# A wait on every indirect DMA of a slot of node rows, instead of on the first of the slot alone

## The chip, the cores and the metric

One core of one Trainium2 chip. The time is the device time of one execution in microseconds (us); less is better. The engines are named as in the profile: PE (TensorE), DVE (VectorE), ACT (ScalarE), POOL (GpSimd) and SP (SyncE).

## What is computed

Sixteen graphs of 1,024 nodes with 64 channels each pass two graph layers. In the first, some edges of a node of high degree are left out, every node sorts, channel by channel, the features of its remaining neighbours and of itself, and a weighted sum of three quantiles of the sorted list (at 0.25, 0.5 and 0.75) is its aggregate. The second is three dense graph convolutions. Both are added to their input after a layernorm. Cut to the core (`neigh` is `adj > 0` without the diagonal):

```python
h = relu(layernorm(x))
# layer 0
rem = neigh & (skip > 1) & (rank % skip == skip - 1) & mask    # then made symmetric
nd = where(rem, 0, adj_with_diagonal) > 0
s = sort(where(nd[..., None], h[:, None], inf), axis=2)
nv = nd.sum(2)
for tau, w in ((.25, .25), (.5, .5), (.75, .25)):
    agg += w * (s interpolated at position tau * (nv - 1))
x = x + (relu((h + agg) @ W1 + b1) @ W2 + b2) * mask
# layer 1
h = relu(layernorm(x))
x1, x2, x3 = bn(relu(adj @ (h @ Wi) + bi)), one after the other
x = x + relu(concat(x1, x2, x3) @ Wl + bl)
```

## The kernel before

The graphs are worked in eight pairs. Within a graph the nodes are put in order of their number of neighbours ("place"), so that nodes of like degree stand together and share one sorting network. Places 0 to 640 and 960 to 1,024 are worked with the channels of two graphs on the partitions (blocks, `BLOCKS` and `TAIL`); PE picks the neighbours' rows by products with selection matrices (L1176, L1247). Places 640 to 960, the **node sets** (`NODES`), are worked with the nodes on the partitions, and their neighbours' rows are fetched from DRAM by indirect DMAs. This is where the change lies.

**A node set.** `fetch_nodes` (its indirect DMA is L1361) makes one tile `g_nodes` of 128 partitions by `slots` x G x 64 values, with G = 2 in every set. There are 17, 19 or 21 slots, a slot being one neighbour of each of 128 nodes, and a slot is filled by two indirect DMAs of 128 rows of 64 values (a = 0 and a = 1). In sets of kinds 0 and 1 the two are the two graphs of a pair; in kind 2 (21 slots) they belong to two different pairs. There are 20 sets and 744 such gathers in all, all issued on POOL's queue. `sort_nodes` then sorts the set on DVE (`quantiles`, L1092 for the min and max steps, L1104 for the products with the coefficients) and the aggregates are stored to DRAM (`agg_d`).

**The condition.** `quantiles` writes the sort operation that it has just put into the program to `sorted_by[0]` (at L1092). `ask()` in `fetch_nodes` adds, to the gather with a = 0 of each slot, a dependency on that operation: the gather may start only when that sort step is done. The gather with a = 1 has no such dependency. The first set's 34 gathers are asked for before there is any sort, and have none.

**What sets the order.** The program is written as generators. `weave` runs one sort and steps other generators beside it, each in a given stretch of the sort (`asking(nodes, 0.0, 0.9)`: its slots are asked for, evenly, over the first 90% of the sort's work). So the source places a gather between certain sort operations. A scheduler then sets the order on each engine: an instruction that waits for nothing may be placed ahead of those in front of it in the source. Sections under `tc.high_priority()` go ahead of others once what they need is there: the sends of image rows (L895, 8 for each graph), the loads of those rows (L910) and the aggregate loads (L1554). On a queue the instructions are issued in the order so set, one after the other.

**The loop over pairs** (about 250 to 2,000 us). For each pair: sort of block 0, a node sort, sort of block 1, sort of block 2, a node sort, at times tails, sort of the last block. Two node sets are fetched and sorted for each pair. Beside the sorts run the gathers of the next block on PE and the preparation of the next pair (`prepare`), in which ACT and PE compute the edges and the places, and POOL sends the image rows (L895) to their places and loads them back (L910).

**The late part** (about 2,000 us to the end). While the last pair's sorts are worked, `later` runs beside them. For each pair p, `load(p)` loads the input, h and the aggregates: the last by 16 indirect DMAs on POOL (L1554), from `agg_d` into the tile `agg`, of which there is one buffer. It is free for the next pair once the layernorm of the pair before (L608) has been transposed on PE (L1440). `first` adds h (L1451, on DVE) and works the dense part of layer 0; `second` the three convolutions (L1509). In this part four node sets are fetched ahead of their sorts (`then`), beside the sorts of blocks 1 and 2, the tails and a node sort.

Of the kernel before, what the change touches and what calls it, by code (L numbers as in the profile page):

```python
# [408 lines left out]
def graph_layers_kernel(ctx: ExitStack, tc: tile.TileContext, ins, out: bass.AP):  # L409
# [641 lines left out]
    sorted_by = [None]  # L1051
# [296 lines left out]
    def fetch_nodes(pairs, i, pools, tag):  # L1348

        work, ps, rows = pools  # L1350
        j0, j1, _, slots = NODES[i]
        G = len(pairs) if i == 2 else 2
        pool = work if tag == "s" else keep if tag == "r0" else rows
        g = pool.tile([P, slots, G * C], F32, tag=tag, bufs=2 if tag == "s" else 1, name="g_nodes")

        def ask():
            for k in range(slots):
                for a in range(G):
                    st = pairs[a if i == 2 else 0]
                    at = 4 if i == 2 else 2 * a + i  # L1360
                    asked = nc.gpsimd.indirect_dma_start(  # L1361
                        out=g[:, k, a * C : (a + 1) * C],
                        out_offset=None,
                        in_=rows_d[st.p][:, :],
                        in_offset=bass.IndirectOffsetOnAxis(ap=st.listed[:, at, k : k + 1], axis=0),
                    )
                    if a == 0 and sorted_by[0] is not None:
                        tc.add_manual_dep(
                            asked.ins, sorted_by[0].ins.name,
                            mybir.DependencyInfo(mybir.DependencyClass.Sync, mybir.DependencyReason.DATA),  # L1370
                            reason="rows are asked for one by one",
                        )
                yield

        z = work.tile([P, len(TAUS), G], F32, tag="z_nodes", bufs=2, name="z_nodes")
        for a in range(G):
            st = pairs[a if i == 2 else 0]
            at = 4 if i == 2 else 2 * a + i
            nc.scalar.copy(z[:, :, a : a + 1], st.nodes_z[:, :, at : at + 1])
        return pairs, i, g, z, Steps(ask())  # L1380

    def asking(fetched, first, end, share=1.0):
# [509 lines left out]
```

## Time and profile before

| | before |
|---|---|
| median of 3 runs | 2845.74 us (2841.83 to 2846.65) |
| the profiled execution's own time | 2855.05 us |
| its span | 2853.2 us |
| mean granted clock of PE | 0.869 |
| node gathers (L1361) on POOL | 744, busy 979.2 us, mean 1,316 ns |
| image rows sent (L895) on POOL | 128, busy 178.7 us, mean 1,396 ns |
| aggregate loads (L1554) on POOL | 128, busy 134.8 us, mean 1,053 ns |
| first addition of a late pair (L1451) on DVE | 8, busy 9.8 us, idle before them 184.1 us |

The profile is one execution. Times are in us from the start of its span. A line of a timeline gives the start, the duration, the engine, the source line, the operation, the tile written and the tiles read, and in square brackets the time that the engine was idle before it and what ended that idle time; "issue" means that nothing shown in the profile was waited for. A line of the waits gives engine, tile and line, what was waited for, the sum in us, how often, and the longest. In the slices, the span is cut into 40 equal parts, and each digit is the busy share in tenths. The span lies 1.9 us below the execution's own time.

### The profile page before, as it was taken

How to read it: one execution, taken by the hardware profiler on the slowest of the kernel's cores; microseconds unless marked ns; L12 is line 12 of the kernel's file. 1: busy time of each engine (PE TensorE's matmuls, PEld its weight loads, DVE VectorE, ACT ScalarE, POOL GpSimd, SP SyncE). 2: the span in 40 equal slices, each digit the busy share in tenths (PEclk: the TensorE clock that was granted, in tenths of full speed). 3: DMA queues.
4: the chain of work that ended last, by engine and by line, in shares of the span. 5: the costliest groups of instructions: out<-in, count | busy, mean ns of one | idle time of the engine just before them, and what ended most of it. 6: DMA issues, size and time to landing. Idle time of an engine off the chain costs nothing. (4 is left out here: it accounts for less than half of the span.)

```text
span 2853.2 us, 54558 instructions
## 1 busy us (share of the span) xinstructions
PE 2127.4 (75%) x21226; PEld 1374.2 (48%) x21226; DVE 2259.9 (79%) x5356; ACT 1657.8 (58%) x3324; POOL 1358.7 (48%) x1155
## 2 busy tenths in 40 slices
PE   1567986897798699779855986997588496448768
PEld 0344563564455365545523553665355363234445
DVE  3117999889899989989999999989688486647843
ACT  2686788678677858867773777687423141122222
POOL 5115363475526416443734274175646748862220
PEclk9788997998899799789878997998798798778989
DMA  3303222322422323142431222322310351221221
GB/s 96 109 30 98 80 88 65 104 80 58 107 72 86 81 91 91 46 110 68 98 65 45 82 86 73 112 75 61 80 21 19 74 82 51 42 56 39 48 61 46
DMA packets 261035, 205.27 MB, mean 72 GB/s; under 512 B 217120, under 2 KB 217248, under 8 KB 256672
## 3 DMA queue, kind: packets, MB, share of 16 engines
q1 hardware_dynamic: 165120, 131.39, 15.5%
q0 software_dynamic: 39680, 62.23, 9.1%
q10 hardware_dynamic: 55968, 8.09, 2.1%
q8 instruction: 168, 2.75, 0.4%
q14 instruction: 99, 0.81, 0.1%
HBM read 148.82 MB, written 52.75 MB: 71 GB/s over the span
## 5 line engine op out<-in xcount | busy, mean ns | idle before, releaser
L1361 POOL DMA_INDIRECT g_nodes<-rows_d,rows_listed x744 | 979.2, 1316 | 952.5 <-DVE prod L1104 276.2
L1176 PE MATMUL pg<-s,hp 128*64 128x496 fp8e4 (+5 forms) x8064 | 747.0, 337 | 134.9 <-ACT hp L697 56.1
L1176 PEld LDWEIGHTS <-hp 128*64 128x64 bf16 x8064 | 450.2, 113 | 376.9 <-ACT hp L697 67.2
L1509 PE MATMUL pg<-adjT,xw 128*64 128x512 fp8e4 x2304 | 282.5, 394 | 24.6 <-ACT xw L1498 11.4
L895 POOL DMA_INDIRECT live_d<-edge,place x128 | 178.7, 1396 | 191.1 <-DVE place L887 154.9
L1151 DVE TENSOR_SCALAR s<-r 128x3200 uint16<-128x3200 uint16 (+2 forms) x192 | 199.6, 1049 | 56.9 <-PE pg L1176 56.8
L1554 POOL DMA_INDIRECT agg<-agg_d,place x128 | 134.8, 1053 | 196.4 <-DMA agg_d<-agg_nodes 118.0
L1509 PEld LDWEIGHTS <-xw 128*64 128x64 bf16 x2304 | 135.4, 113 | 154.1 <-issue 22.8
L782 ACT ACTIVATE edge<-a 128x1024 fp8e4<-128x1024 uint32 x128 | 135.8, 1062 | 105.1 <-DMA a<-in_adj 87.2
L1180 ACT ACTIVATE g<-pg 128x400 f32<-128x400 f32 (+3 forms) x168 | 84.3, 502 | 191.1 <-PE pg L1176 161.3
L1092 DVE TENSOR_TENSOR t<-g 128x800 f32<-128x800 f32 (+9 forms) x184 | 168.0, 926 | 5.4 <-ACT g L1180 3.4
L884 ACT ACTIVATE stays<-keys,minus 128x1024 fp8e4<-128x1024 f32 x128 | 143.6, 1122 | 41.7 <-PE keys L876 40.5
L865 ACT ACTIVATE edge<-q,bias 128x1024 fp8e4<-128x1024 f32 x128 | 142.2, 1112 | 41.6 <-PE q L860 41.6
L838 ACT ACTIVATE stays<-cs,back 128x1024 f16<-128x1024 f32 x128 | 139.1, 1114 | 41.5 <-DVE look L819 19.8
L789 PE MATMUL ptE<-ident_h,one 128*128 128x128 bf16 x1024 | 83.4, 232 | 106.1 <-DVE one L786 58.0
L1092 DVE TENSOR_TENSOR g<-t 128x992 f32<-128x992 f32 (+7 forms) x176 | 160.0, 934 | 2.4
L1451 DVE TENSOR_TENSOR agg<-agg,h_late 128x1024 f32<-128x1024 f32 x8 | 9.8, 1224 | 184.1 <-DMA agg<-agg_d,place 184.1
L930 PE MATMUL pt<-ident_h,lp 128*128 128x128 bf16 x1024 | 107.7, 276 | 60.7 <-ACT liveT L933 33.2
L1247 PE MATMUL pg<-s,hp 128*64 128x384 bf16 (+14 forms) x1872 | 149.1, 301 | 2.8 <-DVE s L1216 2.7
L792 ACT ACTIVATE edgeT<-ptE 128x1024 fp8e4<-128x1024 f32 x128 | 130.8, 1033 | 19.9 <-PE ptE L789 19.6
L1513 ACT ACTIVATE xT<-pg,c_L_gnn_b 128x512 f32<-128x512 f32 x48 | 32.9, 686 | 183.9 <-PE pg L1509 175.3
L786 DVE TENSOR_SCALAR one<-a 128x1024 fp8e4<-128x1024 f32 x128 | 88.5, 696 | 55.6 <-DMA a<-in_adj 45.3
(253 smaller groups left out, 5043.3 us busy)
## 6 DMA issues: line engine op xcount, KB each, us to landing
a<-in_adj SPq DMA_DIRECT2D x128, 512.0 KB
adjT_d<-edgeT SPq DMA_DIRECT2D x16, 1024.0 KB
lp<-live_d POOLq DMA_DIRECT2D x32, 512.0 KB
adjT<-adjT_d SPq DMA_DIRECT2D x16, 1024.0 KB
g_nodes<-rows_d,rows_listed POOLq DMA_INDIRECT x744
room<-in_x SPq DMA_DIRECT2D x16, 256.0 KB
h_d<-room SPq DMA_DIRECT2D x16, 256.0 KB
rows_d<-room SPq DMA_DIRECT2D x64, 64.0 KB
```

What stands on the lines that cost most here:

```text
L782: nc.scalar.activation(edge[:, t, :], a[:, :].bitcast(U32), AF.Sign, accum_out=found[:, 0, b, t : t + 1], saturate=False)
L838: nc.scalar.activation(stays[:, t, :], cs, AF.Abs, bias=back[:, t : t + 1], scale=2.0)
L865: nc.scalar.activation(edge[:, t, :], q, AF.Relu, bias=bias(-2.0), accum_out=nv[:, t : t + 1], saturate=False)
L884: nc.scalar.activation(junk, keys, AF.Sign, bias=minus[:, t : t + 1], accum_out=above[:, t : t + 1], saturate=False)
L895: sent = nc.gpsimd.indirect_dma_start(out=live_d[b][:, :], out_offset=bass.IndirectOffsetOnAxis(ap=place[:, b, t : t + 1], axis=0), in_=ed ...
L1092: sorted_by[0] = nc.vector.tensor_tensor(view(bufs, o, n1, n2), view(bufs, a, n1, n2), view(bufs, b, n1, n2), ALU.max if op else ALU.min)
L1151: nc.vector.tensor_scalar(s[:, j, :, us, :], st.r[0][:, :, us, j0:j1], abs(k - 3), 0x0808, ALU.logical_shift_right if k > 3 else ALU.logic ...
L1176: summed = nc.tensor.matmul(out=pg[x * C : (x + 1) * C, those, :], lhsT=st.hp[:, part, x, u, :], rhs=picked, start=(i == 0 and part == 0), ...
L1247: summed = nc.tensor.matmul(out=pg[x * C : (x + 1) * C, ks, w0:], lhsT=st.hp[:, part, x, u, :], rhs=s[:, ks, x, u, w0:], start=(whole and ...
L1361: asked = nc.gpsimd.indirect_dma_start(out=g[:, k, a * C : (a + 1) * C], out_offset=None, in_=rows_d[st.p][:, :], in_offset=bass.IndirectO ...
L1509: nc.tensor.matmul(out=pg[cs, :], lhsT=part[:, u, cs], rhs=adjT[x][:, u, sl], start=(u == 0 and k == 0), stop=(u == NT - 1 and k == len(xw ...
L1554: nc.gpsimd.indirect_dma_start(out=agg[:, t, x, :], out_offset=None, in_=agg_d[b][:, :], in_offset=bass.IndirectOffsetOnAxis(ap=place[:, b ...
```

## The change

The condition `a == 0` is dropped. Both gathers of a slot, not only the first, get the dependency on the sort operation that stands ahead of them in the source.

```diff
--- before.py
+++ after.py
@@ -1364,7 +1364,7 @@
                         in_=rows_d[st.p][:, :],
                         in_offset=bass.IndirectOffsetOnAxis(ap=st.listed[:, at, k : k + 1], axis=0),
                     )
-                    if a == 0 and sorted_by[0] is not None:
+                    if sorted_by[0] is not None:
                         tc.add_manual_dep(
                             asked.ins, sorted_by[0].ins.name,
                             mybir.DependencyInfo(mybir.DependencyClass.Sync, mybir.DependencyReason.DATA),
```

The instructions themselves are the same in number and kind. Their order is the same on PE, DVE, ACT and SP, and differs on POOL, where the gathers with a = 1 no longer stand ahead of their partners. Between two groups of image rows (L895) there are, in turn, 62 and 10 gathers in the program before, and 52 and 20 in the changed one. Ahead of the eight groups of aggregate loads (L1554) stand, each counted from the group before it (the first from the last load of image rows, L910):

| group of 16 loads | 1 | 2 | 3 | 4 | 5 | 6 | 7 and 8 |
|---|---|---|---|---|---|---|---|
| gathers ahead, before | 28 | 14 | 62 | 27 | 82 | 15 | 0 |
| gathers ahead, changed | 14 | 28 | 51 | 21 | 83 | 31 | 0 |

## The prediction

> **What bounds the kernel now.** I read the page first (engine totals, slices), then VectorE's waits, then the timelines of POOL and VectorE (DVE) around each wait. Totals and slices:
>
> ```profile
> PE 2127.4 (75%) x21226; PEld 1374.2 (48%) x21226; DVE 2259.9 (79%) x5356; ACT 1657.8 (58%) x3324; POOL 1358.7 (48%) x1155
> ...
> DVE  3117999889899989989999999989688486647843
> ```
>
> A slice is 71.3 us. From the fourth to the twenty-sixth (about 210 to 1,850 us) DVE is 80 to 90% and more busy: the loop over pairs is bound by its sorts. From the twenty-eighth on it falls to 40 to 80%. Its waits say why:
>
> ```profile
> DVE agg L1451 <- DMA agg<-agg_d,place: 184.1, 8, 61.5
> DVE s L1151 <- PE pg L1176: 56.8, 27, 5.8
> ```
>
> Eight waits, 184.1 us, all after 2,030 us: VectorE stands before the first addition of each late pair (L1451) until that pair's 16 indirect loads (L1554) have landed. Those loads and the 744 node gathers share POOL's queue, in program order. So in the tail the question is how many gathers stand ahead of a pair's loads. The two views that price this are POOL's timeline around the fourth pair's loads, and DVE's at the waits:
>
> ```profile
> 2325.02 0.97 POOL L1361 DMA_INDIRECT g_nodes<-rows_d,rows_listed  x1 [31.65 <-PE pg L1247]
> ...
> 2352.41 1.09 POOL L1361 DMA_INDIRECT g_nodes<-rows_d,rows_listed  x1 [0.30 <-issue]
> 2353.80 0.94 POOL L1554 DMA_INDIRECT agg<-agg_d,place  x1 [0.30 <-issue]
> ```
>
> ```profile
> 2052.76 1.23 DVE L1451 TENSOR_TENSOR agg<-agg,h_late 128x1024 f32<-128x1024 f32 x1 [18.78 <-DMA agg<-agg_d,place]
> ...
> 2273.74 1.22 DVE L1451 TENSOR_TENSOR agg<-agg,h_late 128x1024 f32<-128x1024 f32 x1 [37.58 <-DMA agg<-agg_d,place]
> ...
> 2375.39 1.22 DVE L1451 TENSOR_TENSOR agg<-agg,h_late 128x1024 f32<-128x1024 f32 x1 [22.71 <-DMA agg<-agg_d,place]
> ...
> 2531.51 1.22 DVE L1451 TENSOR_TENSOR agg<-agg,h_late 128x1024 f32<-128x1024 f32 x1 [61.54 <-DMA agg<-agg_d,place]
> ```
>
> In the first, 17 gathers (2325.0 to 2353.5) run one behind the other, gap 0.30, and the load starts right behind them: the number in brackets is the idle time before an instruction. In the second, the brackets are the stalls. Sixteen loads take 19.7 us (2353.80 to 2373.47) and 22.9 to 25.5 where DVE works beside them.
>
> In the loop the place to read is the start of a node sort: DVE must find all slots there.
>
> ```profile
> 759.53 1.41 POOL L1361 DMA_INDIRECT g_nodes<-rows_d,rows_listed  x1 [16.68 <-DVE g L1092]
> ...
> 776.30 1.19 POOL L1361 DMA_INDIRECT g_nodes<-rows_d,rows_listed  x1 [0.30 <-issue]
> ```
>
> ```profile
> 786.38 1.48 DVE L1092 TENSOR_TENSOR t_nodes<-g_nodes 128x1280 f32<-128x1280 f32 x1
> ```
>
> Eleven gathers, released at 759.3 and done at 777.5; their sort begins at 786.38 without a wait. No wait of DVE on a node gather is in the trace.
>
> **What the skill says.** "Perfetto Trace Analysis", section on SWDGE DMA instructions: the recorded end is the last descriptor, not the data. The trace agrees: loads ended on POOL at 2050.94, DVE went on at 2052.76, 1.8 us later. "DMA: Bandwidth & Descriptors", Anatomy of one DMA: a wait is served by the issuing sequencer before dispatch, so what stands behind on that queue waits too; the 0.30 us gap above agrees. "GPSIMD Engine Reference", Key points: GpSimd shares its SBUF interface with VectorE. The trace agrees: gathers with their gap come at 1.25 us while DVE is idle (32 of them, 2470.3 to 2510.2), at 1.66 while it sorts (759.5 to 777.8), up to 1.93 (2373.8 to 2470.3). No page bears on the order that the scheduler makes.
>
> **The change part by part.** It adds a condition to 372 of the 744 gathers (the second of each slot), less 34 issued before any sort. No instruction is added or removed, and PE, DVE, ACT and SP keep their order. A second gather directly behind its first, on the same queue, waits for nothing new: price nothing by itself. What counts is that POOL's order changes. Before, the scheduler moved the free second gathers ahead in bursts (62 gathers between two sets of image rows, then 10; after, 52 and 20); now each slot's two stand together behind their sort operation.
>
> *(a) Image rows (L895) in the loop.* The even image's come behind 10 fewer gathers, some 11 to 16 us earlier; nobody was late for them. The odd image's wait for their places (L887) either way. Nothing.
>
> *(b) Node sorts in the loop.* The burst ahead is gone, so after the last conditions two gathers per slot are to come.
> - Fifth set (21 slots, sort at 786.4): 22 instead of 11 gathers from 759.5. In 26.9 us at 1.66, 16.2 are done; 5.8 are left while DVE stands, at 1.25: 7.2, and 1.8 to land: **+9.0**.
> - Tenth set (21 slots): POOL is the bound, 42 gathers back to back. The free ones began at 1324.3; the first condition ends at 1328.8. So 4.5 later: 1407.5 + 4.5 + 1.8 = 1413.8 against a sort at 1410.7: **+3.1**.
> - 17-slot sets at 1801.4 and 1555.8: 18 gathers instead of 9. For the first, 1801.4 + 18 x 1.7 + 1.8 = 1833.8 against its first reader of the last slot at 1832.65, and a little for its partner: **+2** for both.
> - The other sets have 1 to over 8 us left by the same sum: 0.
>
> Loop: +14 (from +4, if gathers keep 1.25 and only the fifth and tenth sets are late at half, to +22 at a pace of 1.93).
>
> *(c) The tail*, as shift D of DVE against before, without the loop's:
> 1. First loads: 14 instead of 28 gathers ahead; the last two slots' conditions end by 2018.6, the gathers by 2022.8. Sixteen loads beside a working DVE, 21.5, and 1.8 to land: 2046.1 against 2052.8: D = -6.7.
> 2. The 21-slot set sorted at 2086.65: 22 instead of 11 gathers, condition at 2064.9 - 6.7 = 2058.2, sort due at 2080.0. In 21.8 us at 1.685, 12.9 are done; 9.1 x 1.25 = 11.4, landing 1.8: 2093.2. D = +6.6; this step costs 13.3.
> 3. Second loads hang on the sort itself: D stays.
> 4. Third loads: 51 instead of 62 gathers ahead. The 52nd of before starts at 2238.56; there the loads now begin: 2238.6 + 6.6 + 19.7 + 1.8 = 2266.7 against 2273.74: D = -7.0. The stall of 37.6 becomes 24.
> 5. Fourth loads: the 17 hoisted gathers shown above are gone (counted from the start of the tail 131 gathers stood ahead, now 114). The one buffer agg is free once the layernorm's last step (L608, done at 2334.2) is transposed (L1440), 1.4 later; with D that is 2328.6. Loads 23.8 beside DVE, and 1.8: 2354.2 against 2375.39: D = -21.2. The stall of 22.7 becomes 9.
> 6. Fifth loads: 83 against 82 gathers, POOL back to back: D = -20. The stall stays at 61.
> 7. Sixth loads: 31 instead of 15 gathers ahead, from 2510.5 at 1.515 (2530 to 2553): 2557.5, where they would be ready at 2568.6 - 20 = 2548.6. D = -11.1.
> 8. Seventh and eighth hang on sorts and on their own stores: D stays -11.
>
> Where stalls go: DVE finds work earlier, but the pairs' matmuls (L1509) follow in a fixed row, so I carry D on unchanged.
>
> Sum: +14 - 11 = **+3 us**. The profiled run's own time is 2855.05 (span 2853.2); it becomes 2858. The median of the runs shown is 2845.74, 9.3 below the profiled one; I take the same 3 us from it: **2849**.
>
> **Unknowns, both ends.** The trace of before shows no two-gather burst with DVE reading behind it. Its price lies between nothing (all hidden by work that follows) and 9 + 3 + 2 + 13 = 27 us as worked, 33 at the slowest pace; a gain in the loop is excluded, since no DVE wait on a gather exists there. Landing: 1.8 taken; the larger burst might need 3.
>
> **Rivals.** A measurement of this kernel tells about 0.2% (5.7 us) from no change.
> - *A, the tail's gain stands alone.* The node sorts' lateness is swallowed: DVE has some 3 us of other idle time in every 50 of the loop, which a stall can displace. Then -11, and without step 2 as well -11 - 13 = -24: 2822 to 2835, say 2828. For it: 26% of L1361's idle time hangs on DVE (276.2 of 952.5 us at one line), POOL is 48% busy. Against it: 22 gathers cannot be done in 26.9 - 1.8 = 25.1 us unless each takes 1.14, and the fastest stretch shows 1.25. Chance 0.27.
> - *B, slower: gathers late at every sort behind the first block sort.* The point from which it decides is the pace: 18 gathers between 1801.4 and 1830.9 need 1.64 each. At 1.93, with the doubled burst against a sorting DVE, the fifth set is late by 12, the tenth by 5, and five of the 17- and 19-slot sets by 3 to 4 each: +34; the tail's step 2 costs 15: D = -9. Sum +25: 2871. For it: the paces of 1.92 and 1.75 at those two places (gathers of several us at 1519 to 1547). Against it: 1.58 to 1.66 at 324, 525 and 759. Chance 0.25.
> - *C, the order is not changed at all.* Excluded: POOL's instruction order differs (first burst 62 against 52). Chance 0.
>
> **Chances.** Forecast case 0.48, own range 2837 to 2863; within it about 0.08 faster, 0.20 same, 0.20 slower by that bound. With A and B: faster 0.35, same 0.20, slower 0.45. The range takes in A's middle and B's, and leaves out their ends: 2824 to 2869.
>
> **What would show it.** Right: POOL's timeline shows gathers in twos behind each condition; DVE waits on g_nodes appear (none before), about 9 us at the fifth set and 13 at the set of 2086; L1451's third wait is 24, the fourth 9, the fifth still 61, the sixth about 21. Wrong: no DVE wait on g_nodes (A), or such waits at eight sets or more (B); a fourth wait still near 23 would mean that the loads were not held by the hoisted gathers.

## The result and the profile after

The change makes the kernel slower: 2871.09 us (median of 4 runs, 2867.16 to 2889.58) against 2843.78 (4 runs, 2840.71 to 2846.65). The medians lie 27 us apart; the ratio is 1.0101, with an interval of 1.0067 to 1.0135, which is 19 to 38 us. The forecast was 2849, 3 us slower, with a range of 2824 to 2869. The measured time lies 2 us above that range and the loss is nine times the forecast; the time came out at that of rival B.

The two profiles stand closer than the medians. The changed kernel's profiled execution took 2867.16 (span 2865.3), 4 under its median; that of the kernel before took 2855.05, 11 over its own. Their difference is 12.1. Both numbers are needed below: stalls are read from the traces, the size of an effect from the runs.

The engine totals and DVE's waits of the changed kernel:

```profile
PE 2137.9 (75%) x21226; PEld 1380.6 (48%) x21226; DVE 2262.7 (79%) x5356; ACT 1657.4 (58%) x3324; POOL 1363.2 (48%) x1155
```

```profile
DVE agg L1451 <- DMA agg<-agg_d,place: 160.7, 8, 67.8
...
DVE t_nodes L1092 <- DMA g_nodes<-rows_d,rows_listed: 36.1, 5, 14.7
...
DVE g_nodes L1092 <- DMA g_nodes<-rows_d,rows_listed: 1.1, 1, 1.1
```

Every engine is as busy as before to within 0.5% (DVE 2262.7 against 2259.9); what has moved is idle time. The wait of the late pairs' additions fell from 184.1 to 160.7. In its place stands a wait that the profile before does not have at all: node sorts wait 37 us for their rows. The three longest of these, in DVE's timeline:

```profile
795.29 1.49 DVE L1092 TENSOR_TENSOR t_nodes<-g_nodes 128x1280 f32<-128x1280 f32 x1 [10.01 <-DMA g_nodes<-rows_d,rows_listed]
...
1613.34 1.23 DVE L1092 TENSOR_TENSOR t_nodes<-g_nodes 128x1024 f32<-128x1024 f32 x1 [8.24 <-DMA g_nodes<-rows_d,rows_listed]
...
2117.33 1.49 DVE L1092 TENSOR_TENSOR t_nodes<-g_nodes 128x1280 f32<-128x1280 f32 x1 [14.66 <-DMA g_nodes<-rows_d,rows_listed]
```

And what was won, at the third and fourth pair's additions, with the fifth that grew:

```profile
2289.58 1.25 DVE L1451 TENSOR_TENSOR agg<-agg,h_late 128x1024 f32<-128x1024 f32 x1 [23.62 <-DMA agg<-agg_d,place]
...
2380.87 1.23 DVE L1451 TENSOR_TENSOR agg<-agg,h_late 128x1024 f32<-128x1024 f32 x1 [10.27 <-DMA agg<-agg_d,place]
...
2542.98 1.29 DVE L1451 TENSOR_TENSOR agg<-agg,h_late 128x1024 f32<-128x1024 f32 x1 [67.84 <-DMA agg<-agg_d,place]
```

The brackets were 37.58, 22.71 and 61.54 before. Since DVE runs the same instructions in the same order in both kernels, the start of one and the same instruction can be subtracted between two traces; each jump of this difference is a place where time was lost or won. The shift is +22 when the first late addition is due, +30.7 after the sort at 2117, +15.8 after the third addition, +5.5 after the fourth, +11.5 and +16.2 after the fifth and sixth, and +12 to +13 at the end.

How the first long wait comes about is seen in POOL's timeline at the fifth set, where DVE stands from 785.3 to 795.3:

```profile
785.43 0.94 POOL L1361 DMA_INDIRECT g_nodes<-rows_d,rows_listed  x1 [0.30 <-DVE coef L1104]
...
791.67 0.94 POOL L1361 DMA_INDIRECT g_nodes<-rows_d,rows_listed  x1 [0.30 <-issue]
```

The gathers follow each other with the same gap of 0.30, and six of them were still to come when DVE had nothing left to do: the queue, not the last condition, is late (DVE had finished its last sort step, the last that a condition can name, at 778.9). From 785.4 on, with DVE idle, each takes 0.94; the last ends at 792.6, and 2.7 later the sort begins.

### The profile page after: what moved, and what is told of

It is laid out like the page before. It is cut to its first block, busy times and chain, and to the rows that moved or that the text cites. A ratio compares the mean times of both kernels' runs of the same rounds, so it can differ in the third digit from the quotient of the medians.

```text
span 2865.3 us, 54544 instructions
## 1 busy us (share of the span) xinstructions
PE 2137.9 (75%) x21226; PEld 1380.6 (48%) x21226; DVE 2262.7 (79%) x5356; ACT 1657.4 (58%) x3324; POOL 1363.2 (48%) x1155
## 3 DMA queue, kind: packets, MB, share of 16 engines
q1 hardware_dynamic: 165120, 131.39, 15.5%
## 5 line engine op out<-in xcount | busy, mean ns | idle before, releaser
L1361 POOL DMA_INDIRECT g_nodes<-rows_d,rows_listed x744 | 1005.9, 1352 | 979.8 <-DVE g L1092 298.7
L895 POOL DMA_INDIRECT live_d<-edge,place x128 | 157.5, 1231 | 168.7 <-DVE place L887 126.0
L1554 POOL DMA_INDIRECT agg<-agg_d,place x128 | 134.2, 1049 | 213.1 <-DMA agg_d<-agg_nodes 59.4
L1092 DVE TENSOR_TENSOR t_nodes<-g_nodes 128x256 f32<-128x256 f32 (+6 forms) x192 | 124.7, 659 | 39.8 <-DMA g_nodes<-rows_d,rows_listed 36.1
L1451 DVE TENSOR_TENSOR agg<-agg,h_late 128x1024 f32<-128x1024 f32 x8 | 9.9, 1242 | 160.7 <-DMA agg<-agg_d,place 160.7
```

Of the source, the lines that this page charges most:

```text
L895: sent = nc.gpsimd.indirect_dma_start(out=live_d[b][:, :], out_offset=bass.IndirectOffsetOnAxis(ap=place[:, b, t : t + 1], axis=0), in_=ed ...
L1092: sorted_by[0] = nc.vector.tensor_tensor(view(bufs, o, n1, n2), view(bufs, a, n1, n2), view(bufs, b, n1, n2), ALU.max if op else ALU.min)
L1361: asked = nc.gpsimd.indirect_dma_start(out=g[:, k, a * C : (a + 1) * C], out_offset=None, in_=rows_d[st.p][:, :], in_offset=bass.IndirectO ...
L1554: nc.gpsimd.indirect_dma_start(out=agg[:, t, x, :], out_offset=None, in_=agg_d[b][:, :], in_offset=bass.IndirectOffsetOnAxis(ap=place[:, b ...
```

## The experiments

Theory: the loss is node sorts that stand for their last rows (first fifteen sets), the gain is aggregate loads that no longer stand behind hoisted gathers (last five sets). Rivals: the loss lies in the late part and the single profile hides it; or the loop loses by something other than these waits. The sets are counted by one line, `nth`, in `fetch_nodes`, in the order in which they are fetched, from 0.

**The two halves of the change.**

```diff
-                    if a == 0 and sorted_by[0] is not None:
+                    if (a == 0 or nth >= 15) and sorted_by[0] is not None:
```

```diff
+                    if (a == 0 or nth < 15) and sorted_by[0] is not None:
```

The first has the five late sets in pairs, the second the first fifteen. The order on POOL changes in the half concerned alone; on all other engines it is as before. Both were run on two chips. On the first of them the kernel before takes 3179.40 us; what is different there is told in the last section.

> Both gathers wait only in the five sets of the late part (16th to 20th); the fifteen sets before are as in the kernel before. Theory (the loss is the node sorts that stand for their last rows, the gain the aggregate loads that leave POOL earlier): the stall of 14 us at the 21-slot set of 2086 is gone, no wait of DVE on g_nodes; third loads -14, fourth -12, fifth +6, sixth +5 as in the traces: 12 to 18 us faster than before, about 2829. Rival (the loss is in the late part, which the single profile hides): 5 to 20 us slower than before.

Measured there: 3167.39, ratio 0.9943 (0.9920 to 0.9966).

> Both gathers wait only in the first fifteen sets; the five late ones are as in the kernel before. Theory: 22 us of lateness in the loop, 5 of them won back at the first loads, 14 lost at the set of 2086: 28 to 33 us slower than before, about 2875. Rival (the loss is in the late part): 0 to 12 us slower.

Measured there: 3077.55, ratio 0.9680 (0.9662 to 0.9699). Neither theory had this.

> The late sets alone, once more, since the first four runs came from a chip on which the kernel before takes 3179 and PE stutters in bursts of gathers. On a chip where the kernel before takes about 2844: by the traces 12 to 18 faster (2829), no DVE wait on g_nodes, third and fourth wait of the first addition 24 and 10. On a chip of about 3179: again about 0.6% faster.

Measured, on a chip where the kernel before takes 2846.82: 2829.12, ratio 0.9944 (0.9928 to 0.9959): 17.7 faster. No wait of DVE on g_nodes in the trace.

```profile
2252.48 1.23 DVE L1451 TENSOR_TENSOR agg<-agg,h_late 128x1024 f32<-128x1024 f32 x1 [21.02 <-DMA agg<-agg_d,place]
...
2341.63 1.22 DVE L1451 TENSOR_TENSOR agg<-agg,h_late 128x1024 f32<-128x1024 f32 x1 [10.21 <-DMA agg<-agg_d,place]
...
2500.53 1.22 DVE L1451 TENSOR_TENSOR agg<-agg,h_late 128x1024 f32<-128x1024 f32 x1 [65.26 <-DMA agg<-agg_d,place]
...
2569.55 1.23 DVE L1451 TENSOR_TENSOR agg<-agg,h_late 128x1024 f32<-128x1024 f32 x1 [20.10 <-DMA agg<-agg_d,place]
```

The gain at the third and fourth addition and the loss at the fifth and sixth are those of the change, to within 4 us each.

> The first fifteen sets alone. On a chip where the kernel before takes about 2844: 28 to 33 slower (2875) with four or five DVE waits on g_nodes of some 37 in all, as in the profile of the change. If the loss of the change lies in the late part instead, 0 to 12 slower. On a chip of about 3179: again about 3% faster.

Measured: 2884.09, ratio 1.0146 (1.0124 to 1.0167): 37 slower, more than was expected. DVE's waits for the rows in its trace are 43.7 in all, with 0.7 in a line beside this one:

```profile
DVE t_nodes L1092 <- DMA g_nodes<-rows_d,rows_listed: 43.0, 6, 14.7
```

> The changed kernel beside them on the same chip: 20 to 30 slower than before where that takes about 2844, some 118 faster where that takes about 3179. In both, the sum of the two halves within 8.

Measured: 2875.53, ratio 1.0104 (1.0078 to 1.0129), 28.7 slower on the chip of the two halves. The halves sum to -17.7 + 37.3 = 19.6, 9 short of it, one more than expected. So the loss is all in the first fifteen sets, and the rival that puts it in the late part is refuted.

**Is the loop's loss those waits?**

```diff
+                    if (a == 0 or nth not in (4, 9, 10, 14)) and sorted_by[0] is not None:
```

> The change for all sets but four: in the fifth, tenth, eleventh and fifteenth set (the ones whose sort waited for its rows by over 4 us in some profile) only the first gather of a slot waits, as before. Where the kernel before takes about 2844: if the loss of the loop is those waits, it is gone but for some 6 us of the smaller waits of the third, ninth and thirteenth set: 2833 to 2837, about 0.4% faster than before. If the loss has another cause in the loop (paired gathers that disturb DVE or the transfers of the next pair), 10 us or more of it stay: 2842 and above. Where before takes about 3180: between the two halves, 1% to 3% faster.

Measured: 2838.63 against 2850.39, ratio 0.9963 (0.9948 to 0.9977). DVE's waits on the rows that are left:

```profile
DVE t_nodes L1092 <- DMA g_nodes<-rows_d,rows_listed: 2.7, 1, 2.7
...
DVE g_nodes L1092 <- DMA g_nodes<-rows_d,rows_listed: 0.4, 1, 0.4
```

With 2.8 more before the third set's sort that the trace puts down to no releaser, that is 5.9 us. The late sets alone gave 0.9944; the ratio here is 0.0019 higher, 5.4 us, and the two intervals leave about 6 us either way. So no cost of pairs in the other eleven early sets shows beyond their own waits. Taking four sets out of fifteen turns 1% slower into 0.4% faster: from 1.0104 to 0.9963 is 40 us, by the two intervals 32 to 48, and the waits before these four sorts in the second trace of the change make 9.7 + 6.7 + 4.4 + 14.7 = 35.5. The other rival falls too.

One of the four is not the change's alone. In one trace in which the first fifteen sets are as before (`later_asks_pairs`, below), the tenth set waits 4.57 us for its rows; in the five other traces with this set as before it waits for nothing.

**The queue ahead of the fifth loads.** The late half gained by fewer gathers ahead of a load. The fifth addition still waits 65 us behind 83 of them, though two of the sets fetched there are sorted over 130 us later. So these two were asked for one weave later, once with the late sets in pairs and once with the condition of before, and then, in pairs, later still. The first fifteen sets are as before in all three. The edit of the first two:

```diff
-                sort_pairs(MID + 1, *TAILS[NP - 1], tails, pools), asking(then[1], 0.0, 0.5), asking(then[2], 0.5, 1.0),
+                sort_pairs(MID + 1, *TAILS[NP - 1], tails, pools), asking(then[1], 0.0, 1.0),
...
-            weave(sort_nodes(then[0], pools), asking(then[3], 0.0, 1.0), steps(6))
+            weave(sort_nodes(then[0], pools), asking(then[2], 0.0, 1.0), steps(6))
...
-            weave(sort_pairs(MID, NP - 1, NP, both, pools), steps(7))
+            weave(sort_pairs(MID, NP - 1, NP, both, pools), asking(then[3], 0.0, 1.0), steps(7))
```

(For the third kernel `then[2]` stands beside `sort_pairs(MID, ...)` and `then[3]` beside `sort_nodes(then[1], ...)`.)

> As the run with the late sets alone in pairs, and two of these sets are asked for one weave later, so that 48 instead of 83 gathers stand ahead of the fifth aggregate loads. If the fifth stall of 65 us is POOL's queue alone: 35 gathers of 1.25 less, 44; the sixth loads then stand behind 48 instead of 31, about 20 back: 2800 to 2812. If the stall hangs on something else that is due at the same time, no faster than 2829.

Measured: 2811.36, ratio 0.9866 (0.9846 to 0.9885).

```profile
2464.09 1.22 DVE L1451 TENSOR_TENSOR agg<-agg,h_late 128x1024 f32<-128x1024 f32 x1 [20.89 <-DMA agg<-agg_d,place]
...
2553.23 1.22 DVE L1451 TENSOR_TENSOR agg<-agg,h_late 128x1024 f32<-128x1024 f32 x1 [40.23 <-DMA agg<-agg_d,place]
```

Against the run with the late sets alone, the fifth wait is shorter by 44.4 (44 expected), and the sixth, the longest now, longer by 20.1 (about 20 expected). Both steps came as reckoned. This shows, too, that a load on POOL's queue cannot go before the gathers ahead of it. (The gap of 0.30, which the prediction named for that, shows only that issues follow each other.)

> The same later asks with the condition of the kernel before: 56 instead of 82 gathers ahead of the fifth loads, third and fourth loads as before (62 and 27). By the queue: 32 less at the fifth, 15 back at the sixth: 2826 to 2834, some 20 slower than the same asks in pairs. If waiting in pairs has no part of its own, as fast as those.

Measured: 2826.74, ratio 0.9923 (0.9903 to 0.9943): with the same asks, 15 us behind the pairs. Its third and fourth waits are those of the kernel before, within 3 us, and its fifth is 25.86:

```profile
2278.09 1.23 DVE L1451 TENSOR_TENSOR agg<-agg,h_late 128x1024 f32<-128x1024 f32 x1 [38.86 <-DMA agg<-agg_d,place]
...
2378.23 1.23 DVE L1451 TENSOR_TENSOR agg<-agg,h_late 128x1024 f32<-128x1024 f32 x1 [20.18 <-DMA agg<-agg_d,place]
```

So waiting in pairs has a part of its own in the late sets: with 62 and 27 gathers ahead of these two loads the waits stay, with 51 and 21 they are 20 to 24 and 10.

> The two sets asked for one weave later still: 42 gathers ahead of the fifth loads, 18 of the sixth, 54 of the seventh. By the queue: 51 less at the fifth, nothing back at the sixth, and the seventh loads, which wait for a store of a sort anyway, some 10 later: 2775 to 2800. If the seventh loads are held by the 54 gathers, about 2810.

Measured: 2799.63, ratio 0.9827 (0.9810 to 0.9844). The fifth and the seventh wait:

```profile
2456.29 1.23 DVE L1451 TENSOR_TENSOR agg<-agg,h_late 128x1024 f32<-128x1024 f32 x1 [11.98 <-DMA agg<-agg_d,place]
...
2623.21 1.23 DVE L1451 TENSOR_TENSOR agg<-agg,h_late 128x1024 f32<-128x1024 f32 x1 [25.20 <-DMA agg<-agg_d,place]
```

Against the late sets alone the fifth wait is 12 instead of 65. The seventh is 25 instead of 5, behind 54 gathers: 20 are given back there, where some 10 were expected. This version beats the kernel before by 51 us, and the changed one by some 80, an estimate, since the two did not run on one chip (2850.39 x 1.0104 - 2799.63).

**Second profiles.** On the first of the two chips both kernels were profiled once more:

> The changed kernel once more, for a second profile: waits of DVE on g_nodes of 36 us in five places and 161 us at the first addition of the late pairs if the first profile stands for all runs. If the 27 us of the medians are more than the 12 between the two profiles because a stall varies, this profile shows other sums at the same places.

> The kernel before once more, for a second profile: its first profile came from an execution of 2855 where the median is 2844. If that excess is a late set, a wait of DVE on g_nodes or a longer fifth stall (61.5) shows where 10 us lie; if it is spread evenly or in the clock, no single stall differs by over 3 us.

They took 3061.67 and 3184.70 there, so they say nothing on the 11 us by which the profiled execution before exceeds its median. That excess stays open.

## Why the prediction was wrong

The steps of the forecast's tail, and the change of the wait (the bracket) at each place against the profile before, in two traces of the change (the first, and the one taken beside the two halves) and in that of the late sets alone:

| place | forecast | first trace | second trace | late sets alone |
|---|---|---|---|---|
| first loads | -6.7 | -5.4 | -5.2 | -3.3 |
| set of 2086 | +13.3 | +14.7 | +14.7 | 0 |
| second loads | 0 | 0 | -1.7 | -1.7 |
| third loads | -13.6 | -14.0 | -17.8 | -16.6 |
| fourth loads | -14.2 | -12.4 | -12.5 | -12.5 |
| fifth loads | +1.2 | +6.3 | +3.7 | +3.7 |
| sixth loads | +8.9 | +4.2 | +7.8 | +7.5 |
| seventh loads | 0 | -2.5 | -1.2 | -2.5 |
| sum of the tail | -11.1 | -9.1 | -12.2 | -25.4 |

**The tail (c) was right in its mechanism, and within about 5 us at each step.** What it assumed, that a shift is carried on unchanged, holds within about 2 us in the traces of the change. Its steps at the third to sixth loads, those of the late sets, sum to -17.7; they are -17.9 in the trace of the late sets alone, and the runs of that kernel gave -17.7 (-12 to -20 by the interval). That the digits agree is luck.

One step of the tail is not shown: the first loads. With the fifteenth set as before, and so 28 gathers ahead, the first wait is 12.1 to 15.5 in five other traces (the late sets alone, all but four, the three with later asks), against 18.78 in the profile before. With 14 ahead it is 13.4 to 13.5. So most of the -5 goes with this one profile of the kernel before, and not with the change.

**Step (b) failed, by its size.** The forecast was +14 for the loop. The waits for rows in the loop, each read from the bracket of the sort's operation:

| set | forecast | first trace | second trace | first fifteen alone |
|---|---|---|---|---|
| fifth | 9.0 | 10.0 | 9.7 | 9.8 |
| tenth | 3.1 | 1.4 | 6.7 | 6.4 |
| eleventh and thirteenth | 2 | 8.9 | 5.3 | 10.2 |
| third, ninth, twelfth | 0 | 5.0 | 4.5 | 6.6 |
| sum | 14 | 25.3 | 26.2 | 33.0 |

(The traces put the third set's wait of 2.2 to 3.1 down to no releaser; it stands before the operation that reads the gathered rows, and is counted here.) The price of the fifth set was right. Two terms were mis-sized, and three sets were put at nothing that had such a wait:
- *Landing.* The forecast took 1.8, measured at the aggregate loads. From the end of the last gather to its sort it is 2.7 at the fifth set, 2.6 to 3.4 at the tenth, and 7.4, 5.0 and 7.3 at the eleventh. The Trainium skill ("Perfetto Trace Analysis", DMA Instruction, SWDGE) says that the end in the profile is not the landing; the traces agree, and show that the distance is no constant. At the eleventh set these windows of the change go with the 7.4 (the last three columns are PE's clock, the share of the DMA engines' time in use, GB/s):

```profile
1600.00:1605.00 5.00, 4.73 (x55) 2.74 (x51) 4.67 (x10) 4.20 (x9) 4.09 (x4) 1.00 0.72 227
1605.00:1609.00 4.00, 4.00 (x45) 2.27 (x41) 0.10 (x1) 2.06 (x5) 0.92 (x1) 1.00 0.78 217
```

  The DMA engines are 0.72 to 0.78 in use there, by loads of the adjacency and a store of its transpose; 0.28 is the mean over most of the loop. In the same trace, from 2 us before the end of the last gather to the sort, the share is 0.24 at the fifteenth set and 0.51 at the fifth, where the rows land after 2.6 and 2.7; it is 0.64 at the eleventh and 0.81 at the third, where they take 7.4 and 4.2. That these transfers hold up the rows is argued from this, not tried.
- *The backlog.* The 17-slot sets were priced as 18 gathers from the last conditions on, with an empty queue. At the eleventh set the 17 free gathers of the kernel before had been issued at 1447.7 to 1473, in an empty stretch of POOL. In pairs, all 34 stand behind a first condition at 1534.5 and run to 1605.9, one of them at 10.19. First and last of the free ones before, then first and last of all after:

```profile
1447.67 2.08 POOL L1361 DMA_INDIRECT g_nodes<-rows_d,rows_listed  x1 [19.25 <-DVE prod L1104]
...
1472.18 0.94 POOL L1361 DMA_INDIRECT g_nodes<-rows_d,rows_listed  x1 [0.30 <-issue]
```

```profile
1534.55 3.84 POOL L1361 DMA_INDIRECT g_nodes<-rows_d,rows_listed  x1 [95.26 <-DVE g_pairs L1092]
...
1604.82 1.10 POOL L1361 DMA_INDIRECT g_nodes<-rows_d,rows_listed  x1 [0.30 <-issue]
```

  When the sort step was done that lets the last nine slots go (it ends at 1555.6 before, at 1570.7 after), 21 gathers were left and not 18. They took 35.2, at 1.67 each: the pace was as priced, the queue was three gathers, some 5 us, behind.

The third, ninth and twelfth set were said to have "1 to over 8 us left". They were late by 1 to 3; at the third, and at a later step of the ninth, the rows came 4.2 to 5.9 after the end of the last gather, so a slow landing on a small margin would do it.

**Forecast to runs.** Loop waits of 25 to 26 instead of 14, with the forecast's tail of -11, give +14 to +15. Without the first loads' -6.7, which the traces do not bear out, they give +21 to +22. The runs show 27 and 28.7, by their intervals 19 to 38 and 22 to 37. The 6 us that are left are less than these intervals leave open, and their cause is not known. One candidate: by the third set's sort the second trace and that of the first fifteen sets alone are 5.5 us late, 3.1 to 3.2 of them at a wait for a store of the transposed adjacency (298), where POOL had done the same as before. The run with four sets free again has this wait too (2.9); the first trace of the change does not, nor do the five traces with all of the first fifteen sets as before. Whether the pairs bring it about was not tried.

**The rivals.** A is refuted: the waits are there, and nothing swallowed them. B had the sign and the time (2871), and not the distribution: two 21-slot sets and one of 17 slots carry nearly 80% of the loop's lateness (19.6 of 25.3 in the first trace); the third and ninth have 1.7 to 3.1 each, the thirteenth under 1. For its 1.92 us a gather at 1555.8 the prediction counted 2.8 us in which POOL stood for conditions; the gathers there took 1.36 on the mean. Two small readings of it are off without weight for the sum: 276.2 of 952.5 is 29%, not 26%, and of DVE's slices the fourth reads 7 and the twenty-eighth 9. No cost of the image rows (L895) shows: with four sets free again, the run is, within 6 us, where these waits alone put it.

## What to carry to other kernels

When a wait is added to an instruction on a shared in-order queue, price what the scheduler had put in that place, and not only the wait itself. Work hoisted into an empty stretch of the queue (gathers at 1447 to 1473, needed at 1590) is cover, and should stay free; work hoisted ahead of a transfer on which the busiest engine waits (2325 to 2353) is an obstacle and should be held back. The same edit did both, so ask for it by place: in the late sets alone it gives 0.6% instead of a loss of 1%, and with later asks 1.7%.

## What the runs showed that was not expected

On the first of the two chips the kernel before took 3179.40, 12% more than elsewhere, and the changed one 3061.67: a ratio of 0.9606 (0.9584 to 0.9628). The same edit, on another chip of the kind, has the other sign. DVE is as busy there as elsewhere (2262.4); PE is busy for 2256.6 instead of 2127.4, at a mean granted clock of 0.821 instead of 0.869. And PE stands for what the profile calls issue, which the first profile does not have among PE's longest waits:

```profile
PE pg L1176 <- issue: 81.1, 116, 3.0
...
PE pg L1509 <- issue: 59.0, 35, 3.6
```

PE's timeline in such a stretch (kernel before, that chip), at its longest gap:

```profile
271.43 0.49 PE L1176 MATMUL pg<-s,hp 128*64 128x400 fp8e4 x1 [3.00 <-issue]
```

Matmuls come one by one with gaps of up to 3 us, at a granted clock of 0.50 (254 to 280). Gaps of this kind (over 0.12 us before a matmul that has no wait) were summed from the traces over stretches with more than 2 us of them. By where a stretch is cut, they make 147 to 164 us in the kernel before and 75 to 94 in the changed one, whose gathers come in smaller bursts. POOL was busy with its DMAs for 0.54 to 0.85 of the time in these stretches. In the first stretch, at the first set's gathers, which no condition touches, both kernels have about the same (21 to 22). On the other chips the traces looked at (before, after, the two halves) have no such stretch. The gaps are under half of the 335 us by which this chip is slower, and some 70 of the 118 between the two kernels on it. What makes that chip stutter, whether the bursts cause it, and where the rest lies was not tried; a figure for this kernel holds for a chip that is named with it.
